# Two graph layers fused on one Trainium2 core: the order of work between the steps, where layer 1 begins, beside its matmuls and in the last rows

## The chip, the core and the metric

The kernel runs on one NeuronCore of a Trainium2 chip. Five engines run side by side, each with its own queue of instructions, taken in order: TensorE (PE) does the matmuls and the transposes, VectorE (DVE) and ScalarE (ACT) work on vectors, GpSimd (POOL) does small vector work, and SyncE (SP) issues DMA transfers. ACT and POOL issue transfers too. Engines wait for each other through semaphores. The metric is the device time of one execution in microseconds (us), as the median of several runs.

## The reference

A graph has N = 2708 nodes with D = 256 features and a random sparse adjacency `adj` (weights from 0.05 to 1, the diagonal set in the mask). Layer 0 adds two kinds of propagation, two steps each; layer 1 is a graph attention layer with four heads of 64 features. Both are followed by a layernorm with a residual.

```python
# layer 0
R = S + eye(N);  R = R / R.sum(-1, keepdims=True)
Z, Xf, Xa = 0, X, X
for n in range(2):
    A  = top_p_attention(Xa, W1, W2, W3)   # softmax(q @ k.T), the rows' largest entries
                                           # up to a mass of 0.9, renormalised
    Xf = R @ Xf
    Xa = A @ Xa
    Z  = Z + Xf @ U1[n].T + Xa @ U2[n].T
h = layernorm(X + Z) * ln_g + ln_b
x = layernorm(x + h)
# layer 1
Wh  = einsum('nd,hdo->nho', x, W)
e   = leaky_relu(s_i[:, None, :] + s_j[None, :, :], 0.2)   # s_i, s_j from Wh and a
att = softmax(where(adj != 0, e, -inf), axis=1)
x   = layernorm(x + einsum('ijh,jho->iho', att, Wh).reshape(N, 256))
```

## The kernel before

The nodes lie in NT = 22 row tiles: 16 of 128 rows and 6 of 110. All is float32. A fast way is computed always. A flag, `bad`, says at the end whether the data kept to the fast way's assumptions; if not, a general way follows inside `tc.If`. With this input it isn't entered.

**Layer 0.** For each tile there is a *walk* (`walks`, L901: 22 matmuls of one tile of the adjacency with `xe` or, in step 1, `xm`) into a single PSUM buffer, and an attention row: logits (`scores`, L661), a search for the top-p threshold on DVE, ACT and POOL (`search`: MAX8 at L766, MATCH_REPLACE8 at L786 and L832), turning the weights by PE transposes (`turned`, L240) with an ACT copy (L245), and the matmuls with them (`weigh`, L258). The end of a walk is an add on DVE that frees the PSUM buffer: `after_walk0` with `xf` (L915) in step 0, `finish` with `xw` (L974) in step 1. `step(s, ...)` goes over the 22 tiles of a step; between groups of source tiles it calls `slot`. A slot first advances the searches in progress (`going`) and the endings of earlier tiles (`doing`), and then issues a number of walk matmuls; `SPEND_BETWEEN` is 7 pieces of work of the stream. Between step 0 and step 1 there is a stretch of slots alone, in which the rest of step 0's walks and the first three searches of step 1 are done.

At the end of a tile of step 1, `finish` adds the terms, `norms` does the two layernorms, and `sources` computes what layer 1 needs of the tile: transposes (L160) and matmuls (L166) on PE, then `sb`, `tj`, `s_src` and `v` (the tile `cs`, L176) on ACT, and `v` goes to DRAM (L179). The last LATE = 4 tiles (18 to 21) have their norms and sources done later, beside layer 1's matmuls. For them a second form of the layernorm, `layernorm_beside`, has the sums made on ACT and one-column arithmetic on POOL (L146 to L151), and ACT applies it (L153). The multiply by the gain and the add of the residual are 256 wide on POOL (L187, L188).

**Layer 1.** The targets are taken in three groups of 8, 8 and 6 tiles (`spans`). For each group all 22 source tiles are gone over in pairs. Per source tile SP loads a block of the adjacency, ACT turns it into a mask (`neighbours`: Sign at L1221, Square at L1222), DVE sets the diagonal where the tile is among the targets (L1225), and DVE makes four weight tiles `pt`, one for each head (`weights`, L1302: one scalar_tensor_tensor of 1024 columns, three sets of buffers). PE then does 16 `values` matmuls per pair (L1313) and 16 `denominators` matmuls of `pt` with `sb` (L1323; counts for a group with two chunks of 512 columns). `beside` is called twice a pair, ahead of the values and behind the denominators. It advances the late tiles (`prepared`), `verdict` (which computes `bad` in some 17 small DVE operations, a matmul and a DVE operation) and the outputs of the group before (`settle`).

Once the last group is done, `settle` runs for its six tiles alone, in a staggered row: PE transposes (L1234), a reciprocal `rden` on DVE (L1236), the multiplication by it (odd tiles on DVE at L1242, even ones on ACT at L1247), the residual add on POOL (L1252), statistics on DVE (L1259 to L1261), the power and `nb` on POOL (L1262, L1263), the output on ACT (L1265), and the store. Then each engine loads the flag from `bad` (L1422) and branches (L1423).

From step 0 on the instructions of PE, ACT, DVE and POOL run in the order in which the program text issues them (`manual_schedule`); only SP's queue is put in order by the planner. So the place of a line in the text is its place in the engine's queue, and an instruction that waits holds up what is behind it.

Of the kernel before, what the change touches and what calls it, by code (L numbers as in the profile page):

```python
# [16 lines left out]
P = 128  # L17
# [27 lines left out]
def kernel(  # L45
# [71 lines left out]
    LATE = 4  # L117
# [63 lines left out]
    def norms(t, xt, norm=layernorm, other=None):  # L181

        m = rows[t]
        hh = xe[:m, t, 0:D]
        h2 = hh if other is None else other()[:m]
        yield from norm(h2, hh, m)
        nc.gpsimd.tensor_mul(h2, h2, g_sb[:m])  # L187
        nc.gpsimd.tensor_add(h2, h2, xt[:m])  # L188
        yield
        yield from norm(hh, h2, m)  # L190
        yield
        if t < NT - LATE:
            yield
# [23 lines left out]
    def spread(g, r):  # L217

        lines = shared[g].rearrange("(t h) m -> h t m", h=H)
        n = len(spans[g]) * rows[spans[g][0]]  # L220
        for k in range(2):
            for h in range(2):
                nc.sync.dma_start(
                    r[k][:, h, :n].rearrange("p (t m) -> p t m", t=len(spans[g])),
                    lines[2 * k + h].partition_broadcast(P),
                )

# [297 lines left out]
    def fast_layer0(ep, adjp):  # L525
# [463 lines left out]
        going, doing, unfinished, stored = [], [], set(), set()  # L989
        ready, held = {}, {}  # L990
# [8 lines left out]
        def slot(spend, begin=None):  # L999

            advance(going)
            if begin and begin[1] < NT:
                going.append(search(*begin))
                next(going[-1])
            advance(doing)
            owed[0] += spend
            while owed[0] > 0:
                owed[0] -= 1
                if next(stream, True):
                    break  # L1010

        def step(s, cur, spend):
            first = None
            for t in range(NT):
# [11 lines left out]
                def between(n):  # L1026
                    last = n == len(groups) - 1
                    if last:
                        xa = heldp.tile([P, D], F32, name="xa1")
                        nc.scalar.activation(xa[:m], ac[:m, :D], AF.Copy, scale=rden)  # L1030
                        if s and t in c3:
                            nc.gpsimd.dma_start(c3[t][:m], xa[:m])
                            stored.add(t)
                        elif s:
                            held[t] = xa
                        else:
                            doing.append(after_attention0(t, xa))
                    slot(spend[n], (s, t + 3) if n == len(groups) - 2 else None)

                def turn_next(n):  # L1040
# [5 lines left out]
                first = weigh(  # L1046
                    ac[:m, :D], first or turn_next(0), m,
# [46 lines left out]
        with tc.manual_schedule(engines=engines):  # L1094
# [22 lines left out]
            for t in range(3):  # L1117
                for n in range(6):
                    slot(SPEND_BETWEEN, None if n else (1, t))
                    if (t, n) == (2, 2):  # L1120
                        break
# [63 lines left out]
        return ahead, verdict  # L1185
# [7 lines left out]
    def layer1(ep, adjp, r=None, verdict=None):  # L1193
# [9 lines left out]

        first = list(range(GT, NT - LATE)) + list(range(GT)) + list(range(NT - LATE, NT))

# [7 lines left out]

        def neighbours(g, j):

            k = rows[j]
            i0, i1 = off[spans[g][0]], off[spans[g][-1] + 1]
            bar = adjp.tile([P, NT - HT, P], F32, name="blk")
            bar = bar.rearrange("p t d -> p (t d)")[:k, : i1 - i0]
            nc.sync.dma_start(bar, adjT[off[j] : off[j + 1], i0:i1])  # L1220
            nc.scalar.activation(bar, bar, AF.Sign)  # L1221
            nc.scalar.activation(bar, bar, AF.Square)  # L1222
            if j in spans[g]:
                own = bar[:, off[j] - i0 : off[j + 1] - i0]
                nc.vector.tensor_tensor(own, own, ident[:k, :k], op=ALU.max)  # L1225
            return bar

        def settle(g, t, val, den, u, last):
# [11 lines left out]
            sums = u[:m, 0:2, :].rearrange("p q (h o) -> p (q h) o", h=2)  # L1240
            if last and t % 2:
                nc.vector.tensor_tensor(  # L1242
                    res[:m], sums, rden[:m].unsqueeze(2).to_broadcast([m, H, FO]), op=ALU.mult
                )
# [6 lines left out]
            flat = res[:m].rearrange("p h o -> p (h o)")  # L1251
            nc.gpsimd.tensor_add(flat, flat, xe[:m, t, 0:D])  # L1252
# [33 lines left out]
        def mask(n):  # L1286
            if n < len(order):
                g, _, j = order[n]
                if g == 0:
                    nc.scalar.dma_start(  # L1290
                        v[j][: rows[j]].rearrange("p h o -> p (h o)"), vd[j][: rows[j]]
                    )
                masks[n] = neighbours(g, j)
# [36 lines left out]
        def prepared(t):  # L1330

            yield from norms(
                t, x_late[:, t - NT + LATE, :], layernorm_beside,
                lambda: pp.tile([P, D], F32, name="h2", bufs=4),
            )
# [4 lines left out]
        if verdict:  # L1340
            late += [[2 * k, prepared(NT - LATE + k)] for k in range(LATE)]
            late.append([2 * LATE, verdict(aux)])
        rest, running = [], []
        def beside(g, i):
# [25 lines left out]
        for n in range(0, len(order), 2):  # L1370
# [13 lines left out]
            for u in (n, n + 1):  # L1384
                for k in range(2):
                    values(u, (2 * k, 2 * k + 1))
                    if last and u > n:
                        for c, (c0, w) in enumerate(cuts[g]):
                            copy = nc.scalar.copy if c == 0 else nc.vector.tensor_copy
                            copy(val[:, k, c0 : c0 + w], acc[k][c][:, :w])  # L1390
            for u in (n, n + 1):
# [7 lines left out]
            else:  # L1399
                beside(g, i + 1)  # L1400
            weights(n + 3)
            mask(n + 4)
        assert not late

# [9 lines left out]

    with ExitStack() as both:
# [6 lines left out]
    flag = nc.values_load(bad[0:1, 0:1])  # L1422
    with tc.If(flag > 0):  # L1423
# [50 lines left out]
```

## Time and profile before

| | |
|---|---|
| Median of 3 runs | 1587.1 us (1586.86 to 1587.92) |
| Profiled execution | 1586.25 us |
| Its span, first to last instruction | 1584.4 us |
| Mean granted PE clock | 0.993 |
| PE busy | 1537.4 us, 97% |
| DVE busy | 1201.2 us, 76% |
| ACT busy | 799.5 us, 50% |
| POOL busy | 440.9 us, 28% |
| Step 0's rest and first searches of step 1 | about 466 to 514 us |
| Layer 1's first matmul | 1225.22 us |
| Layer 1's last matmul of the weights ends | 1561.66 us |

All numbers on the profile come from one profiled execution. The busy shares say which engine has least to spare. The list of waits has, for each pair of instruction and releaser, the sum of idle time, how often it came, and the longest. The chain follows the work that ended last back from releaser to releaser. In the rows of a stretch, the numbers in brackets count instructions, and the next column is the granted PE clock, where 1.00 is full speed. In the timeline a row has start, duration, engine, line, operation, tiles and shapes, and in square brackets the idle time before it.

### The profile page before, as it was taken

How to read it: one execution, taken by the hardware profiler on the slowest of the kernel's cores; microseconds unless marked ns; L12 is line 12 of the kernel's file. 1: busy time of each engine (PE TensorE's matmuls, PEld its weight loads, DVE VectorE, ACT ScalarE, POOL GpSimd, SP SyncE). 2: the span in 40 equal slices, each digit the busy share in tenths (PEclk: the TensorE clock that was granted, in tenths of full speed). 3: DMA queues.
4: the chain of work that ended last, by engine and by line, in shares of the span. 5: the costliest groups of instructions: out<-in, count | busy, mean ns of one | idle time of the engine just before them, and what ended most of it. 6: DMA issues, size and time to landing. Idle time of an engine off the chain costs nothing. (4 is left out here: it accounts for less than half of the span.)

```text
span 1584.4 us, 23826 instructions
## 1 busy us (share of the span) xinstructions
PE 1537.4 (97%) x8029; PEld 1036.2 (65%) x8029; DVE 1201.2 (76%) x3651; ACT 799.5 (50%) x1462; POOL 440.9 (28%) x884
## 2 busy tenths in 40 slices
PE   8999999999998999999999999999998989999994
PEld 4477777776776888787778788887786323333342
DVE  4686776777309767877779888888883888999895
ACT  3444444444345455555645566656643454456473
POOL 2200000100023122232223544444541750044133
PEclk9999999999999999999999999999999999999998
DMA  6100000000144333332333444333343335334231
GB/s 163 61 12 13 9 13 9 9 11 11 43 114 105 100 84 102 80 89 72 85 89 95 110 109 109 104 99 93 91 101 110 110 110 161 95 107 133 81 100 43
DMA packets 172495, 128.27 MB, mean 81 GB/s; under 512 B 44342, under 2 KB 161804, under 8 KB 172362
## 3 DMA queue, kind: packets, MB, share of 16 engines
q1 hardware_dynamic: 162000, 111.86, 26.4%
q0 software_dynamic: 3648, 9.26, 1.7%
q10 hardware_dynamic: 6714, 5.54, 1.1%
q8 instruction: 65, 1.06, 0.3%
q14 instruction: 68, 0.56, 0.1%
HBM read 111.78 MB, written 13.46 MB: 79 GB/s over the span
## 5 line engine op out<-in xcount | busy, mean ns | idle before, releaser
L245 ACT COPY eT<-tr 128x512 f32<-128x512 f32 (+5 forms) x264 | 141.3, 535 | 287.5 <-PE tr L240 284.9
L686 ACT ACTIVATE junk<-e,minus,rth 128x2708 bf16<-128x2708 f32 (+1 forms) x88 | 232.8, 2646 | 36.1 <-POOL rth L718 35.2
L258 PE MATMUL att<-xm,eT 128*128 128x256 f32 (+3 forms) x968 | 230.9, 380 | 0.4 <-ACT xa L1030 0.4
L258 PE MATMUL att<-ba,eT 128*128 128x256 f32 (+3 forms) x968 | 230.8, 379 | 0.3 <-ACT eT L245 0.2
L901 PE MATMUL walk<-xe,blk 128*128 128x257 f32 (+3 forms) x968 | 225.3, 384 | 5.0 <-DVE xf L915 5.0
L901 PE MATMUL walk<-xm,blk 128*128 128x256 f32 (+3 forms) x968 | 222.0, 380 | 1.0 <-DVE xw L974 1.0
L1313 PE MATMUL acc<-pt,v 128*64 128x512 f32 (+3 forms) x1056 | 213.7, 548 | 4.5 <-DVE pt L1302 4.1
L901 PEld LDWEIGHTS walk<-xe,blk 128*128 128x128 f32 (+3 forms) x968 | 178.5, 187 | 50.3 <-issue 12.6
L1302 DVE SCALAR_TENSOR_TENSOR pt<-e,tj,blk 128x1024 f32<-128x1024 f32 (+3 forms) x176 | 185.5, 1122 | 20.7 <-ACT blk L1222 16.0
L901 PEld LDWEIGHTS walk<-xm,blk 128*128 128x128 f32 (+3 forms) x968 | 177.7, 186 | 34.4 <-issue 4.9
L258 PEld LDWEIGHTS att<-xm,eT 128*128 128x128 f32 (+3 forms) x968 | 169.6, 186 | 22.1 <-ACT xa L1030 0.8
L258 PEld LDWEIGHTS att<-ba,eT 128*128 128x128 f32 (+3 forms) x968 | 169.5, 186 | 22.0 <-ACT eT L245 0.8
L665 ACT ACTIVATE e<-lg 128x1024 f32<-128x1024 f32 (+1 forms) x132 | 121.0, 921 | 110.6 <-PE lg L661 107.0
L1313 PEld LDWEIGHTS acc<-pt,v 128*64 128x64 f32 (+1 forms) x1056 | 74.7, 137 | 132.9 <-issue 109.4
L766 DVE MAX8 cand<-e 128x8 f32<-128x170 f32 (+1 forms) x352 | 89.6, 324 | 90.5 <-ACT e L665 90.4
L240 PEld LDWEIGHTS tr<-ident,e 128*128 128x128 f32 (+3 forms) x968 | 115.1, 138 | 56.3 <-issue 21.0
L240 PE MATMUL tr<-ident,e 128*128 128x128 f32 (+3 forms) x968 | 147.1, 271 | 0.7 <-ACT xe L952 0.3
L1302 DVE SCALAR_TENSOR_TENSOR pt<-r,tj,blk 128x1024 f32<-128x1024 f32 (+1 forms) x88 | 109.8, 1312 | 6.1 <-PE acc L1323 3.2
L1323 PE MATMUL acc<-pt,sb 128*32 128x512 f32 (+3 forms) x1056 | 106.8, 545 | 0.0
L766 DVE MAX8 cand<-scr 128x8 f32<-128x97 f32 (+1 forms) x616 | 102.3, 246 | 0.0
L915 DVE TENSOR_TENSOR xf<-walk,xe 128x257 f32<-128x257 f32 (+1 forms) x22 | 9.4, 426 | 110.6 <-PE walk L901 110.6
L784 DVE MAX8 top<-work 128x8 f32<-128x128 f32 (+3 forms) x242 | 82.4, 340 | 8.3
(237 smaller groups left out, 1966.9 us busy)
## 6 DMA issues: line engine op xcount, KB each, us to landing
blk<-in_adjT_dram SPq DMA_DIRECT2D x32, 704.0 KB
blk<-in_adjT_dram SPq DMA_DIRECT2D x32, 512.0 KB
blk<-in_adjT_dram SPq DMA_DIRECT2D x48, 330.0 KB
blk<-in_adjT_dram SPq DMA_DIRECT2D x32, 320.0 KB
blk<-in_adjT_dram SPq DMA_DIRECT2D x12, 605.0 KB
blk<-in_adjT_dram SPq DMA_DIRECT2D x12, 440.0 KB
blk<-in_adjT_dram SPq DMA_DIRECT2D x18, 283.6 KB
c<-cs POOLq DMA_DIRECT2D x32, 128.0 KB, 2.0
```

The costliest lines, as they stand in the source:

```text
L240: nc.tensor.transpose(tr[: rows[t], q, :m], e[:m, off[t] : off[t + 1]], ident[:m, :m])
L245: copy(eT[:k, : len(grp), :m], tr[:k, : len(grp), :m])
L258: nc.tensor.matmul(acc, eT[: rows[t], q, :m], value(t), start=(t == 0), stop=(t == NT - 1),)
L665: nc.scalar.activation(halves[:m, :, c0 : c0 + w], lg[:m, :, :w], AF.Exp, accum_out=zp[:m, n : n + 1],)
L686: nc.scalar.activation(junk[:m], e[:m], func, scale=rth, bias=minus1[:m], accum_out=acc)
L766: nc.vector.max(cand[:, n, :], src[:m, n * size : min(N, (n + 1) * size)])
L784: nc.vector.max(top[:, k : k + 8], work if k else flat)
L901: nc.tensor.matmul(ac[:m, :w], blk[: rows[j], j - j0, :m], cur[: rows[j], j, 0:w], start=(j == 0), stop=(j == NT - 1),)
L915: nc.vector.tensor_add(xf[:m], ac[:m, : D + 1], xe[:m, t, :])
L1302: nc.vector.scalar_tensor_tensor(pt[:k, :gw], targets[g][h // 2][:k, h % 2, :gw], tj[:k, j, h : h + 1], bar, op0=ALU.max, op1=ALU.mult,)
L1313: nc.tensor.matmul(acc[h // 2][c][q * FO : (q + 1) * FO, :w], v[j][:k, h, :], probs[n][h][:k, c0 : c0 + w], **at,)
L1323: nc.tensor.matmul(acc[2][c][h * 32 : (h + 1) * 32, :w], sb[:k, j, h : h + 1].to_broadcast([k, 32]), probs[n][h][:k, c0 : c0 + w], **at,)
```

## The change

1. **Between the steps.** `slot` has an argument `walk_first`. With it, the walk's matmuls are issued ahead of the searches' parts. It is set in the stretch between the steps.
2. **LATE is 3.** Tile 18 gets its norms and sources in layer 0.
3. **The first masks.** `neighbours` moves out of `layer1`, and the first two are called in the last tile of step 1. The loads of `v` for the first three source tiles go to SP's queue.
4. **The late tiles' norms** (`prepared`). Statistics, gain and residual are on DVE; the power alone is on POOL; `nb` is on DVE, three steps of `beside` later; ACT applies it.
5. **`beside`'s second call** in a pair comes between the values and the denominators.
6. **`verdict`** starts 26 steps of `beside` in (NT + 4) where it was 8.
7. **The last rows.** For odd tiles, the multiplication and the residual add are four scalar_tensor_tensor operations of 64 columns on DVE; POOL's add is left out for them.
8. **The flag** is loaded into registers inside `layer1`, ahead of the last rows on PE, ACT, DVE and POOL. SP's load isn't held in the written order.

```diff
-    LATE = 4
+    LATE = 3
...
-        def slot(spend, begin=None):
-            advance(going)
-            if begin and begin[1] < NT:
-                going.append(search(*begin))
-                next(going[-1])
-            advance(doing)
+        def slot(spend, begin=None, walk_first=False):
+            def search_parts():
+                advance(going)
+                if begin and begin[1] < NT:
+                    going.append(search(*begin))
+                    next(going[-1])
+                advance(doing)
+            if not walk_first:
+                search_parts()
             owed[0] += spend
             while owed[0] > 0:
                 owed[0] -= 1
                 if next(stream, True):
                     break
+            if walk_first:
+                search_parts()
...
+                    if s and (t, n) == (NT - 1, len(groups) - 2):
+                        early.extend(neighbours(0, j, adjp) for j in first[:2])
                     slot(spend[n], (s, t + 3) if n == len(groups) - 2 else None)
...
-                    slot(SPEND_BETWEEN, None if n else (1, t))
+                    slot(SPEND_BETWEEN, None if n else (1, t), True)
...
             if last and t % 2:
-                nc.vector.tensor_tensor(
-                    res[:m], sums, rden[:m].unsqueeze(2).to_broadcast([m, H, FO]), op=ALU.mult
-                )
+                for h in range(H):
+                    nc.vector.scalar_tensor_tensor(
+                        res[:m, h, :], sums[:, h, :], rden[:m, h : h + 1],
+                        xe[:m, t, h * FO : (h + 1) * FO], op0=ALU.mult, op1=ALU.add,
+                    )
...
-            nc.gpsimd.tensor_add(flat, flat, xe[:m, t, 0:D])
+            if not (last and t % 2):
+                nc.gpsimd.tensor_add(flat, flat, xe[:m, t, 0:D])
...
-                    nc.scalar.dma_start(
+                    (nc.sync if n < DEEP else nc.scalar).dma_start(
                         v[j][: rows[j]].rearrange("p h o -> p (h o)"), vd[j][: rows[j]]
                     )
-                masks[n] = neighbours(g, j)
+                masks[n] = early[n] if n < len(early) else neighbours(g, j, adjp)
...
         def prepared(t):
-            yield from norms(
-                t, x_late[:, t - NT + LATE, :], layernorm_beside,
-                lambda: pp.tile([P, D], F32, name="h2", bufs=4),
-            )
+            m = rows[t]
+            xt = x_late[:m, t - NT + LATE, :]
+            hh = xe[:m, t, 0:D]
+            h2 = pp.tile([P, D], F32, name="h2", bufs=LATE)[:m]
+            for src, dst in ((hh, h2), (h2, hh)):
+                if src is h2:
+                    nc.vector.tensor_mul(h2, h2, g_sb[:m])
+                    nc.vector.tensor_add(h2, h2, xt)
...
+                nc.vector.bn_stats(st, src)
+                nc.vector.bn_aggr(mv, st)
+                nc.vector.tensor_scalar(ve, mv[:, 1:2], LN_EPS, None, op0=ALU.add)
+                nc.gpsimd.tensor_tensor(rs, ve, minus_half[:m], op=ALU.pow)
+                yield
+                yield
+                yield
+                nc.vector.tensor_scalar(nb, mv[:, 0:1], rs, -1.0, op0=ALU.mult, op1=ALU.mult)
+                yield
+                nc.scalar.activation(dst, src, AF.Identity, scale=rs, bias=nb)
+                yield
             yield from sources(t, pp, aux, nc.scalar)
...
-            late.append([2 * LATE, verdict(aux)])
+            late.append([NT + 4, verdict(aux)])
...
+            if not last:
+                beside(g, i + 1)
             for u in (n, n + 1):
                 denominators(u)
...
-            else:
-                beside(g, i + 1)
             weights(n + 3)
             mask(n + 4)
         assert not late
+        if verdict:
+            flag.append(nc.values_load(bad[0:1, 0:1]))
...
-    flag = nc.values_load(bad[0:1, 0:1])
-    with tc.If(flag > 0):
+    with tc.If(flag[0] > 0):
```

## The prediction

> **What bounds the kernel now.** I read the page's busy shares first, then the list of waits, then the chain inside layer 1, then single stretches.
>
> ```profile
> PE 1537.4 (97%) x8029; PEld 1036.2 (65%) x8029; DVE 1201.2 (76%) x3651; ACT 799.5 (50%) x1462; POOL 440.9 (28%) x884
> ```
>
> TensorE (PE) sets the time: idle in only 47 us of 1584.4. A change can win only from PE's idle time, from PE running at a lower clock, from PE work removed, or from the tail behind the last matmul. The list of PE's waits shows which idle times the diff can touch:
>
> ```profile
> PE aux L160 <- ACT xe L153: 6.5, 3, 2.2
> PE walk L901 <- DVE xf L915: 5.0, 3, 3.2
> PE acc L1313 <- DVE pt L1302: 4.1, 1, 4.1
> ```
>
> 6.5 us three times 2.2, in layer 1's first group; 5.0 us between the steps (0.52, 1.31, 3.18 at 466.5, 489.5 and 503.5); 4.11 us once, where layer 0 passes to layer 1 (1221.11 to 1225.22). The chain shows how a 2.2 arises (start, us, what):
>
> ```profile
> 1269.74 3.57 PE acc L1323 x32
> 1273.32 1.09 PE aux L166 x4
> ...
> 1274.71 0.85 ACT cs L176 x4
> ...
> 1275.59 0.29 ACTq L179
> ...
> 1275.93 0.61 ACT xe L153
> ...
> 1276.58 0.41 PE aux L160 x2
> ```
>
> One tile's source matmuls (L166) come after the pair's denominators (L1323). Next on PE come the following tile's transposes (L160), whose rows ACT finishes (L153) only after the five small copies and the store of the tile before. PE stands idle from 1274.39 to 1276.58.
>
> Last, busy time by stretch (sum, PE, PEld, DVE, ACT, POOL, then PE's clock, DMA):
>
> ```profile
> 490.00:512.00 22.00, 18.00 (x73) 13.51 (x74) 21.13 (x81) 11.53 (x13) 6.87 (x15) 0.92 0.41 109
> 1225.00:1236.00 11.00, 10.65 (x40) 3.93 (x44) 11.00 (x11) 5.89 (x9) 1.47 (x2) 0.85 0.38 114
> 1328.00:1400.00 72.00, 72.00 (x425) 22.22 (x423) 67.91 (x63) 34.03 (x51) 4.42 (x7) 1.00 0.35 104
> ```
>
> After two gaps PE ran at half clock for 3.41 us (508.00 to 511.41, 1224.80 to 1228.21): some 1.7 us each. In group 1 PE is full and DVE has only 4 us in 72 to spare.
>
> **Between the steps: 3.6 us.** Each walk waits for the add (L915) that clears the one walk accumulator. Before, that add stands behind search parts on DVE, and a new walk follows on PE at once. With the walk put first in a slot, PE runs logits after three of the walk ends (1.99 us for 512 columns, 0.83 for 330), which cover an eviction of 0.5. By hand from these rows and a walk matmul of 0.4425 us, three waits remain: 0.52, about 0.5, and about 2.1 where the add falls into the replacing chain (seven MATCH_REPLACE8, 3.8 us, 494.15 to 497.96); together 3.1 in place of 5.0. The last lies between 0.5 (DVE free) and 4.6 (behind the 28 MAX8). So 1.9 are saved, and 1.7 of half clock if 2.1 keeps the clock. No walk matmul is added. The first search ends some 5 us later (506 for 501), still before its tile is turned. Bounds: -1 to +4.
>
> [...] the two throttles begin 716.8 us apart, 210 windows, so the edges are known. Window 504.59 to 508.00 was idle only 2.11 us and was throttled; window 1303.31 to 1306.72 was idle 1.83 and was not. [...] by the rows a 2.1 or 2.65 us gap may cost 1.7 according to its phase. I take none for the first and price the second below.
>
> **Layer change.** Tile 18's norms and sources move into layer 0 (LATE 3): PE gets 1.1 us there (L160 0.2, L166 0.9) and loses about 1.4 in group 0, in which one tile costs 0.34 + 1.09. DVE's added 2.3 us lie in its 4.08 us of idleness at 1191.15. POOL's order moves tile 19's sums by about 3.5 us, with nothing due on them; tile 18's store on SP goes ahead of the second mask load, about 2.4 us late and still landed near 1210, long before it is read. The Sign and Square of the first masks (four of 1.05 us) ran at 1221.70, after the last attention; now ACT does them during the last tile. A third mask's pair stands ahead of the last two turned copies: its load is issued after the last walk near 1213.1, landed near 1216.7 (3.5 us as the other masks), so PE may lose 0 to 0.2. v's loads for the first three tiles move from ACT's queue to SP's and wait, as before, for the end of attention. First weight then about 1222.45 for 1223.88; PE idle from 1222.3 to about 1224.95, 2.65 for 4.11.
>
> **Group 0.** The late tiles' norms go from ACT and POOL to DVE: a half is bn_stats 0.43, aggregate 0.18, add 0.15, later ln_nb 0.18, and the second has two 256-wide operations of 0.42 (as L1242): 2.75 us per tile, 8.3 for three. POOL keeps only the power; it loses the multiply and adds of 0.73, and ACT no longer waits 9.4 us for lb_nb. L166 comes before 3.57 us of denominators, which hide ACT's chain of 2.2: the three stalls, 6.5 us, go. What is late next is DVE: a weight has a pitch of 1.196 us, 8 per pair 9.57, against PE's 10.59 (values 7.02, denominators 3.57). Pairs 3 to 5 carry about 2, and 0.7 of diagonal maxima from then on. DVE's sum up to the sixth pair's weights is 1222.45 + 48 x 1.196 + 7.7 + 0.7 + 1.3 [...] = 1289.5. PE follows by 0.4 + 3.57 + 1.43, so pair 6 ends at about 1294.5, pair 7 (10.59 + 1.43) at 1306.3, pair 8 at 1318.0; before, it ended at 1327.92. So 9.9 us for layer change and group 0. A half clock in pair 1 mostly vanishes in this sum, as DVE sets it.
>
> [...]
>
> ```profile
> 1234.98 12.96 POOL L149 TENSOR_SCALAR lb_sq<-lb_sq 110x1 f32<-110x1 f32 x1 [6.13 <-ACT h L148]
> 1248.02 0.57 POOL L150 TENSOR_TENSOR lb_rs<-lb_sq,minus_half 110x1 f32<-110x1 f32 x1
> ...
> 1254.58 1.50 POOL L150 TENSOR_TENSOR lb_rs<-lb_sq,minus_half 110x1 f32<-110x1 f32 x1
> ```
>
> A one-element operation took 12.96 us while weights ran back to back, and finished when DVE paused. ln_nb on DVE now waits for such a power, with all later weights queued behind it and PE behind those. By the row the cover, three half pairs or 16 us, exceeds 12.96 and five of six cost nothing[...]. I take the 1.3 above and keep 0 to 4.
>
> **Group 1: -1.0.** The verdict (about 17 small DVE operations of 0.18 to 0.31, 3.7 us) moves to pairs 3 to 6 of group 1, where DVE has some 0.6 per pair and its lead: 0 to 2 lost.
>
> **Tail: 1.3.** Behind the last matmul (1561.66) POOL paces the six tiles:
>
> ```profile
> 1571.02 0.64 POOL L1252 TENSOR_TENSOR res<-res,xe 110x256 f32<-110x256 f32 x1
> 1571.61 0.55 POOL L1262 TENSOR_TENSOR ln_rs<-ln_ve,minus_half 110x1 f32<-110x1 f32 x1
> 1572.26 0.26 POOL L1263 TENSOR_SCALAR ln_nb<-ln_mv,ln_rs 110x1 f32<-110x1 f32 x1
> ```
>
> About 1.55 us a tile. Three adds of 0.7 go (2.1). DVE in exchange has four operations of 110x64 for one of 0.42; not in the trace, they lie between 0.17 (110x4) and 0.28 (the search's 128x56 of this kind). At 0.25, DVE's sum from 1562.8 is 6 x 0.85 + 3 x 1.0 plus waits, ending near 1571.3 for 1572.51: 1.2 saved, between 0 and 2. The span ends with POOL: its branch at 1573.82, a drain of 6.69 us to 1583.54. The flag's load on POOL (0.49, half of it on the path) is ahead now: 0.25 saved. On PE (0.49) it lies in the 0.6 us wait for den's copies, on ACT and DVE (0.66, 0.55) it may push rden by 0.15. SP's load stays, its chain done 2.6 us before POOL's. Together 1.3.
>
> **Sum.** 3.6 + 9.9 - 1.0 + 1.3 = 13.8. The profiled execution took 1586.25 (span 1584.4, 1.85 around it), 0.85 under the median 1587.1; taken off the median: **1573.3 us**.
>
> **The rivals.**
> 1. DVE becomes layer 1's bound more than summed: powers at 0.66 each (2.7 over my 1.3), verdict 2.0. For it: 94% busy DVE in group 1, the 12.96. Against it: the cover. About 1578.
> 2. Between the steps nothing is won: the adds fall behind MAX8 chains, the half clock stays. For it: DVE busy 21.13 of 22. Time 1577.
> 3. No change within 0.2%: DVE's pause costs in group 0 what the L160 stalls did, and the tail is fixed by a drain that doesn't move: 1585 to 1588.
> 4. Slower: the ln_nb waits. If POOL's power isn't served while DVE waits for it, or its queue is late, each of the six stops DVE, and PE with it. It decides from 13.8/6 = 2.3 us each; at 3 us, 1591. Against it: POOL has little else left there, and the power took 0.57 with DVE paused.
> 5. Better than summed: weights stretch less without POOL's 256-wide work, clock kept throughout: 1567.
>
> **How the numbers follow.** As summed, 0.63, with its own range 1569 to 1577; rival 1 0.18, rival 2 0.08, rival 3 0.03, rival 4 0.03, rival 5 0.05. 0.2% (3.2 us) is about what a measurement of this kernel can tell from no change. The range reaches to rival 1 with two costs at their bounds and to rival 5: 1567 to 1581. Faster 0.94 (all but 3 and 4), same 0.03, slower 0.03.
>
> **What would show it.** The L160 wait gone from PE's list; walk waits near 3 us; one wait of about 2.6 at the layer change, with or without a half clock; pair 8's end near 1318 less the earlier gains; PE waits on L1302 in pairs 4 to 6 of 2 to 3 us; POOL's branch about 1.5 us sooner behind the last matmul. Wrong if DVE waits for ln_rs by microseconds, if group 1 shows PE waiting for weights in every pair, or if the last turned copies wait for the third mask.

## The result, and the profile after

The changed kernel takes 1576.47 us (median of 4 runs, 1574.92 to 1576.54), the kernel before beside it 1587.34 us: a ratio of 0.9929, with a 95% interval from 0.9912 to 0.9946. On another chip it took 1574.76 us, ratio 0.9926 (0.9913 to 0.9940). So 11 us were won where 13.8 had been forecast, and the time lies inside the range of 1567 to 1581. The changed kernel's nine runs lie either at 1574.3 to 1574.9 us or at 1576.4 to 1577.0, by PE's granted clock (see the last section), so smaller differences between kernels are read here from traces. The profiled execution took 1574.92 us, its span 1573.1 us, which is 11.3 us below the span before.

The change adds lines ahead of the ones the forecast spoke of: the walk is L916 now (L901 before), the attention matmul L273 (L258), the turned copy L260 (L245), the weights L1314 (L1302), the values L1325 (L1313), the denominators L1335 (L1323).

The page's busy shares after:

```profile
PE 1536.7 (98%) x8029; PEld 1037.0 (66%) x8029; DVE 1208.0 (77%) x3698; ACT 791.8 (50%) x1428; POOL 411.9 (26%) x850
```

and the head of the list of PE's waits (us in total, times, longest):

```profile
PE tr L625 <- DMA xa<-in_w1T_dram: 4.9, 1, 4.9
PE att L273 <- ACT eT L260: 3.8, 1, 3.8
PE acc L1325 <- DVE pt L1314: 2.7, 1, 2.7
PE walk L916 <- DVE xf L930: 2.3, 3, 1.3
```

The three waits for L153 are gone (6.5), the layer change fell from 4.1 to 2.7, and the walks' waits from 5.0 to 2.3, which is less than the 3.1 forecast. The first line is the load of the weights at the start, 4.8 us before. The second is a wait that was not there before: the first attention matmul of step 1 waits 3.8 us for its turned copy. PE's busy time hardly changed, so all of this is a matter of waits, of the clock and of the rows behind the last matmul.

Where the time moved shows best at points that both traces have (us from the span's start, PE unless said otherwise; the last pair's end is that of its last matmul in the timeline, 0.2 us behind the 1561.66 of the forecast, where the chain leaves it):

| point | before | after | after less before |
|---|---|---|---|
| first walk's end between the steps | 466.53 | 465.63 | -0.90 |
| a walk's wait in mid step 1 begins | 903.54 | 903.46 | -0.08 |
| last attention matmul's end | 1221.11 | 1222.97 | +1.86 |
| layer 1's first matmul | 1225.22 | 1225.67 | +0.45 |
| pair 8 ends | 1327.92 | 1320.15 | -7.77 |
| pair 33, the last, ends | 1561.86 | 1554.38 | -7.48 |
| POOL's branch | 1573.82 | 1564.73 | -9.09 |
| POOL's drain begins | 1576.85 | 1565.29 | -11.56 |
| span ends | 1584.4 | 1573.1 | -11.3 |

The 0.9 us at the start lie in the first 20 us (loads of the weights and PE's slow first stretch: a matmul of `lg` with `ident` took 0.42 us in it and 0.27 behind it, in both traces, and the records of PE's clock, which begin with full speed, begin at 13.07 before and at 11.23 after); nothing of the change is there, and in the repeat of the changed kernel the same point came at 466.61, so this part is a difference from run to run. Between the steps 0.8 us were lost, not 3.6 won: from the first walk's end to the wait in mid step 1 it took 437.0 us before and 437.8 after, and 439.0 in the repeat, where the half clock that follows lasted twice as long. The stretch from the middle of step 1 to the end of pair 8 brought 7.7, the last rows 3.8.

### The profile page after: what moved, and what is told of

Its sections match the earlier page's. It is cut to its first block, busy times and chain, and to the rows that moved or that the text cites. A ratio compares the mean times of both kernels' runs of the same rounds, so it can differ in the third digit from the quotient of the medians.

```text
span 1573.1 us, 23768 instructions
## 1 busy us (share of the span) xinstructions
PE 1536.7 (98%) x8029; PEld 1037.0 (66%) x8029; DVE 1208.0 (77%) x3698; ACT 791.8 (50%) x1428; POOL 411.9 (26%) x850
## 4 chain that ended last, share of the span: by engine, by line
PE 92%; DVE 4%; ACT 1%; POOL 1%; issue 1%; DMA 0%; ACTq 0%; POOLq 0%; DVEq 0%
PE att L273 25%; PE walk L916 25%; PE acc L1325 13%; PE lg L676 7%; PE acc L1335 7%; PE tr L255 6%; PE tr L961 2%; PE tr L975 2%; PE tr L646 1%; PE tr L166 1%; DVE pt L1314 1%; ACT junk L701 1%; DVE scr L847 0%; DVE scr L766 0%; PE aux L1242 0%
## 5 line engine op out<-in xcount | busy, mean ns | idle before, releaser
L260 ACT COPY eT<-tr 128x512 f32<-128x512 f32 (+5 forms) x264 | 141.2, 535 | 276.9 <-PE tr L255 274.3
L701 ACT ACTIVATE junk<-e,minus,rth 128x2708 bf16<-128x2708 f32 (+1 forms) x88 | 232.8, 2646 | 35.9 <-POOL rth L733 35.1
L273 PE MATMUL att<-ba,eT 128*128 128x256 f32 (+3 forms) x968 | 231.3, 380 | 3.8 <-ACT eT L260 3.8
L273 PE MATMUL att<-xm,eT 128*128 128x256 f32 (+3 forms) x968 | 230.9, 380 | 0.4 <-ACT xa L1052 0.4
L916 PE MATMUL walk<-xe,blk 128*128 128x257 f32 (+3 forms) x968 | 224.9, 384 | 2.3 <-DVE xf L930 2.3
L916 PE MATMUL walk<-xm,blk 128*128 128x256 f32 (+3 forms) x968 | 222.0, 380 | 1.5 <-DVE xw L989 1.5
L1325 PE MATMUL acc<-pt,v 128*64 128x512 f32 (+3 forms) x1056 | 214.0, 549 | 2.9 <-DVE pt L1314 2.7
L916 PEld LDWEIGHTS walk<-xe,blk 128*128 128x128 f32 (+3 forms) x968 | 178.3, 186 | 47.6 <-issue 12.0
L916 PEld LDWEIGHTS walk<-xm,blk 128*128 128x128 f32 (+3 forms) x968 | 177.6, 186 | 35.1 <-issue 4.9
L1314 DVE SCALAR_TENSOR_TENSOR pt<-e,tj,blk 128x1024 f32<-128x1024 f32 (+3 forms) x176 | 184.4, 1113 | 13.6 <-PE att L273 8.7
L273 PEld LDWEIGHTS att<-ba,eT 128*128 128x128 f32 (+3 forms) x968 | 169.6, 186 | 25.6 <-ACT eT L260 4.3
L273 PEld LDWEIGHTS att<-xm,eT 128*128 128x128 f32 (+3 forms) x968 | 169.6, 186 | 22.1 <-ACT xa L1052 0.8
L1325 PEld LDWEIGHTS acc<-pt,v 128*64 128x64 f32 (+1 forms) x1056 | 75.7, 137 | 132.0 <-issue 108.3
L1314 DVE SCALAR_TENSOR_TENSOR pt<-r,tj,blk 128x1024 f32<-128x1024 f32 (+1 forms) x88 | 109.8, 1311 | 3.0 <-PE acc L1335 1.3
L1335 PE MATMUL acc<-pt,sb 128*32 128x512 f32 (+3 forms) x1056 | 106.8, 545 | 0.0
L236 ACT ACTIVATE blk<-blk 128x1024 f32<-128x1024 f32 (+3 forms) x66 | 63.3, 958 | 81.4 <-DMA blk<-in_adjT_dram 66.6
L930 DVE TENSOR_TENSOR xf<-walk,xe 128x257 f32<-128x257 f32 (+1 forms) x22 | 9.4, 426 | 117.0 <-PE walk L916 117.0
```

The source lines that it names most:

```text
L260: copy(eT[:k, : len(grp), :m], tr[:k, : len(grp), :m])
L273: nc.tensor.matmul(acc, eT[: rows[t], q, :m], value(t), start=(t == 0), stop=(t == NT - 1),)
L701: nc.scalar.activation(junk[:m], e[:m], func, scale=rth, bias=minus1[:m], accum_out=acc)
L916: nc.tensor.matmul(ac[:m, :w], blk[: rows[j], j - j0, :m], cur[: rows[j], j, 0:w], start=(j == 0), stop=(j == NT - 1),)
L1314: nc.vector.scalar_tensor_tensor(pt[:k, :gw], targets[g][h // 2][:k, h % 2, :gw], tj[:k, j, h : h + 1], bar, op0=ALU.max, op1=ALU.mult,)
L1325: nc.tensor.matmul(acc[h // 2][c][q * FO : (q + 1) * FO, :w], v[j][:k, h, :], probs[n][h][:k, c0 : c0 + w], **at,)
```

## The experiments

**The slots between the steps.** The changed kernel with this part undone:

```diff
-                    slot(SPEND_BETWEEN, None if n else (1, t), True)
+                    slot(SPEND_BETWEEN, None if n else (1, t))
```

> The changed kernel with the slots between the steps in the old order (searches' parts ahead of the walk). Theory (the walk-first order saves 2.7 us of walk waits and the half clock behind them, and gives 3.75 us and a half clock back where the first turned copy of step 1 stands behind a search's pass on ACT): the waits 0.5, 1.3 and 3.2 us for L930 come back, the wait of PE for the turned copy goes, and the time is 0.8 us lower than the changed kernel's, about 1575.6. Rival (the order pays, and the turned copy is late for another reason): the 3.75 us wait stays and the time is 2 to 4 us above, 1578.5 to 1580.5.

It took 1574.58 us (1574.35 to 1575.14), ratio to before 0.9922 (0.9905 to 0.9938). The waits for L930 are back at 5.0 in total, and the 3.8 us wait for the turned copy is gone. So the wait belongs to the new order, and the new order costs at least as much as it wins: from the first walk's end to mid step 1 this kernel took 437.0 us, as before. Whether the cost is the 0.8 us of the traces, the times alone can't tell.

The chain of the changed kernel between 507 and 515 shows what holds the copy up (start, us, what):

```profile
507.14 0.82 ACT e L680 x2
...
508.09 2.17 POOL fact L688
...
511.28 0.40 ACT rth L718
...
511.70 2.74 ACT junk L701 x2
514.44 0.48 ACT eT L260
...
514.96 2.41 PE att L273 x8
```

With the walk first, parts of the searches stand behind the last slot's matmuls, directly ahead of step 1. One of these parts is a pass over a whole row on ACT (`tally`, L701), which waits for a small chain on POOL. ACT takes its instructions in order, so the two copies for step 1's first tile, ready to go at 511.2, wait for POOL and then for the pass. PE has nothing else to do and stands from 511.21 to 514.96. Then comes a half clock, from 516.40 to 519.81.

If that is the cause, the parts of the last slot need only come after the copies. The next kernel lets the last slot issue its walk alone; its parts follow in step 1's first slot:

```diff
-        def slot(spend, begin=None, walk_first=False):
+        def slot(spend, begin=None, walk_first=False, parts=True):
...
-            if walk_first:
+            if walk_first and parts:
                 search_parts()
...
-                    slot(SPEND_BETWEEN, None if n else (1, t), True)
+                    slot(SPEND_BETWEEN, None if n else (1, t), True, (t, n) != (2, 2))
```

> The changed kernel in which the last slot between the steps issues its walk alone; the searches' parts of that slot come in step 1's first slot, behind the first turned copies. Theory: PE's wait for the turned copy (3.75 us at 511) falls under 1 us, no half clock follows, step 1 begins 4 to 5 us sooner, and the time is about 1571.7. Rival (the pass on ACT only moves in front of the next turned copy): the wait appears at the third copy with 2 us or more, gain under 2 us, 1575.

It took 1571.34 us (1570.75 to 1572.15), ratio 0.9901 (0.9885 to 0.9918). Its timeline (start, us, engine, line, operation, tiles, shapes, count, idle before) has the copies ahead of the pass, and PE idle for only 0.24 us:

```profile
511.10 1.07 ACT L260 COPY eT<-tr 128x512 f32<-128x512 f32 x2 [2.86 <-PE tr L255]
512.05 0.40 ACT L718 ACTIVATE rth<-slope,nguess,y 128x1 f32<-128x1 f32 x1
512.49 2.64 ACT L701 ACTIVATE junk<-e,minus,rth 128x2708 bf16<-128x2708 f32 x1
```

```profile
511.74 1.99 PE L273 MATMUL att<-ba,eT 128*128 128x256 f32 x8 [0.24 <-ACT eT L260]
```

The walks' waits stay at 2.3, no half clock follows, and layer 1 begins at 1220.59 in place of 1225.67. From the first walk's end to mid step 1 it took 432.6 us, 4.4 less than before: this is what the forecast, at 3.6, had meant for this part. At the end 1.0 us is lost again, since POOL's branch took 1.65 us here (see below).

**The parts of layer 1's first group, one by one.** Four kernels, measured by one quantity that neither the start nor the tail touches: from layer 1's first matmul to the end of pair 11. Before it is 134.46 us, in the changed kernel 126.25. The quantity has a spread of its own: six other traces with the changed kernel's group 0 lie at 126.2 to 126.4, but the kernel before with only the flag moved took 136.18, since a half clock, 1.7 us, followed one of its waits for L160.

`beside_only` is the kernel before with one edit:

```diff
+            if not last:
+                beside(g, i + 1)
             for u in (n, n + 1):
                 denominators(u)
...
-            else:
-                beside(g, i + 1)
```

> The kernel before with the second call of beside ahead of the denominators and nothing else. Theory (each L160 stall is ACT's chain between two tiles, which 3.57 us of denominators cover): the three waits of 2.2 us for ACT xe L153 fall below 0.3 each, the loss of 2.1 us in pair 3 stays, and the time is 6.5 us lower, 1580.5. Rival (ACT is late for its wait on POOL, so the waits only move): half of it or less, 1583.5 or above.

1580.75 us, ratio 0.9962 (0.9948 to 0.9976). No wait for L153 is left. The stretch took 129.76 us, 4.7 less: of the 6.5 of stalls, 2.1 came back in pair 9 (12.67 us in place of 10.59), where DVE waits for a mask that ACT makes late, as in pair 3. DVE's waits between 1225 and 1345:

```profile
DVE pt L1302 <- ACT blk L1222: 4.6, 2, 4.1
DVE blk L1225 <- ACT blk L1222: 4.5, 2, 4.1
```

Of the 5.8 us between the two profiled executions, 1.2 are the start's run-to-run difference. The time fits the theory, the sum within it only in part.

`prepared_only` is the kernel before with the new `prepared` alone, four late tiles, `beside` in its old place.

> The kernel before with the late tiles' norms on DVE (four tiles) and nothing else. Theory: pair 3 no longer loses 2.1 us, as DVE's weights don't wait for a mask held up on ACT; the L160 waits stay, one for each pair of tiles, with 1.5 to 2.2 us; DVE's extra 11 us lie inside them. 2 us lower, 1585. Rival (DVE becomes the bound by this part alone): PE waits for the weights in pairs 4 to 7 by over 3 us beside the L160 waits, and the time is 1587 or above.

1587.56 us, ratio 1.0001 (0.9992 to 1.0010). The stretch took 138.82 us, 4.4 more than before, of which 1.7 is a half clock that followed one of the waits for L160: these three waits stay, pair 3 is at PE's pace as the theory had it, but pairs 4 to 6 take 11.4 to 13.1 us each, at DVE's pace. The rival holds. That the time is no worse comes from the tail, told of below.

`both_only` is the kernel before with both.

> The kernel before with the norms on DVE and beside ahead of the denominators, without the other parts (LATE stays 4, masks late). Theory (the gain of layer 1's first group comes from these two alone, less what DVE's bound takes): no L160 waits, 2 to 4 us lost to weights in pairs 4 to 8, 6 to 7 us lower than before, 1580.5. Since DVE carries four tiles in place of three and starts 1.4 us later than with early masks, it stays 1 to 2 us short of the 7.8 us which the changed kernel wins there. Rival (LATE or the masks bring most of it): under 4 us, 1583 or above.

1580.60 us, ratio 0.9958 (0.9944 to 0.9972); the stretch 131.67 us, 2.8 less than before, though 1.9 more than with `beside` alone. Both traces have the same half clock in pair 1 and none later. The norms on DVE cost more than they were moved to save.

`old_norms` asks the same from the other side: the changed kernel, three late tiles and all else, with `prepared` as it was (and `norms` with the arguments that it needs).

```diff
-            m = rows[t]
-            xt = x_late[:m, t - NT + LATE, :]
...
-                nc.scalar.activation(dst, src, AF.Identity, scale=rs, bias=nb)
-                yield
+            yield from norms(
+                t, x_late[:, t - NT + LATE, :], layernorm_beside,
+                lambda: pp.tile([P, D], F32, name="h2", bufs=4),
+            )
```

> The changed kernel with the late tiles' norms as before (sums on ACT, one-column work and the 256-wide operations on POOL, application on ACT), still three tiles and beside ahead of the denominators. Theory (on DVE the norms cost 2.4 us of waits for weights in pairs 4 to 6; on ACT and POOL they hold two masks up by 2.1 us each): from the end of pair 1 to that of pair 11 about 114.5 us in place of 112.7, pairs 4 to 6 at PE's pace, two others 2.1 us long; 1.9 us slower at that point. POOL's stream is longer, so its branch may take 2.9 us again and add 2.1. Rival (the move to DVE brings nothing, DVE is the bound because of it): pair 11 ends 1 us or more sooner than in the changed kernel.

1574.29 us, ratio 0.9921 (0.9904 to 0.9937); the stretch 125.76 us, 0.5 below the changed kernel. I had expected 1.9 more; it is the rival that comes nearer. DVE's waits between 1239 and 1330, first of the changed kernel:

```profile
DVE blk L240 <- ACT blk L237: 2.4, 1, 2.4
DVE pt L1314 <- PE acc L1335: 1.3, 1, 1.3
```

and of the kernel with the old norms:

```profile
DVE pt L1316 <- PE acc L1337: 4.3, 3, 2.1
DVE blk L242 <- ACT blk L239: 3.6, 1, 3.6
DVE pt L1316 <- ACT cs L176: 1.2, 1, 1.2
```

DVE has 9.1 us of slack in place of 3.7, and PE loses 1.6 us in one pair (pair 9, 12.16 us), where DVE waits for a late mask. With the other parts in place, the norms' engine makes next to no difference. Of the 5.4 us between `both_only` and the changed kernel, the third late tile, the later verdict and the earlier first weights have not been told apart.

`masks_late` takes the two early masks out of the last tile:

```diff
                     if s and (t, n) == (NT - 1, len(groups) - 2):
-                        early.extend(neighbours(0, j, adjp) for j in first[:2])
+                        pass
```

> The changed kernel with its first masks made in layer 1 as before (loads and all else as changed). Theory (DVE's start sets the end of group 0): ACT's Sign and Square of mask 0 come behind attention, DVE's first weight starts 2 us later, near 1225, and pair 8 ends as much later as DVE starts: 1.5 to 2.5 us above the changed kernel, 1578.5. Rival (the first matmul waits for v's load and ACT's copy anyway, and PE sets the group): under 0.5 us, 1576.5.

1574.29 us, ratio 0.9919 (0.9903 to 0.9936). Both theories miss. The trace shows ACT making the first two masks in the last tile all the same, at 1210.63 and 1216.39, which is even sooner than in the changed kernel (1217.51 and 1220.58). So the written order holds inside layer 0 and inside layer 1, but ACT's first work of layer 1 stood ahead of layer 0's last copies here: across that border ACT did not keep the order of the text, which the description of the kernel gives for everything from step 0 on. The two lines in the last tile add nothing: from the first matmul to pair 11 the kernel took 126.37 us. In the kernel before, the load of `v` on ACT's queue came ahead of the first mask, at 1221.15, and waited for the end of attention; that its move to SP's queue is what frees the masks is likely, and was not tried alone. The first matmul came 2.56 us after attention, by this row:

```profile
PE acc L1325 <- DMA v<-v: 2.6, 1, 2.6
```

The load of `v` is issued when attention ends, and here its landing is what the layer change waits for. In the changed kernel the list names the weights instead; but the first weight was done at 1224.35, 1.3 us before the first matmul, so that `v` is the likely cause there too.

**The last rows and the branch.** POOL's branch took 2.94 us to POOL's next instruction before, 0.47 after. The forecast had the branch unchanged. The branch and the next instruction (duration in ns, first and last start in us), first before, then after:

```profile
L1423 POOLq COMPARE_BRANCH  x1: 45/45/45, 1573.8 to 1573.8; - x1
L1423 POOLq EVENT_SEMAPHORE  x1: 17/17/17, 1576.8 to 1576.8; - x1
```

```profile
L1457 POOLq COMPARE_BRANCH  x1: 45/45/45, 1564.7 to 1564.7; - x1
L1457 POOLq EVENT_SEMAPHORE  x1: 17/17/17, 1565.2 to 1565.2; - x1
```

Two kernels ask why. One is the kernel before with the flag's load moved up, the other the changed kernel with 34 small POOL instructions more at the start.

```diff
         assert not late
+        if verdict:
+            flag.append(nc.values_load(bad[0:1, 0:1]))
...
-    flag = nc.values_load(bad[0:1, 0:1])
-    with tc.If(flag > 0):
+    with tc.If(flag[0] > 0):
```

> The kernel before with the flag's load ahead of the last rows and nothing else. Theory A (POOL's branch was quick in the changed kernel because its instructions lie at other places in the stream): the branch on POOL still takes 2.9 us to the next instruction, the gain is the load alone, 0.2 to 0.3 us, 1587. Theory B (the early load makes the branch quick): the branch takes 0.5 us, POOL's drain starts 2.7 us sooner, and the time is 1584.5.

1586.68 us, ratio 0.9997 (0.9988 to 1.0006), no change that can be told. The branch took 3.07 us.

```diff
     LATE = 3
+    filler = const.tile([P, 1], F32, name="filler")
+    for _ in range(34):
+        nc.gpsimd.memset(filler, 0.0)
```

> The changed kernel with 34 one-column memsets on POOL at the start, as many instructions as its POOL stream is shorter by. Theory A (place in the stream): POOL's branch takes 2.9 us again in place of 0.47, POOL's drain ends the program again, and the time is 2.1 us above the changed kernel's (2.5 less the 0.38 that POOL waits for SP's end), 1578.6. Theory B (the early load): the branch stays at 0.5 us and the time within 0.5 us, 1576.5.

1578.25 us, ratio 0.9942 (0.9925 to 0.9958); the branch took 2.83 us again, and from the last matmul to the span's end it took 20.8 us in place of 18.8. So the early load has no part in it: with 34 instructions more at the start of POOL's stream the branch went from 0.47 us to 2.83. By which place in the stream this goes was not told apart. All runs, by the number of POOL records ahead of the branch:

| kernels | POOL records ahead of the branch | branch to next, us |
|---|---|---|
| defer | 1093 | 1.65 |
| after, masks_late, slots_old, settle_old | 1094 to 1097 | 0.47 |
| prepared_only, both_only | 1102 | 0.47 |
| combined, old_norms | 1116 and 1117 | 0.47 to 0.48 |
| pad34, flag_only, before, beside_only | 1128 to 1131 | 2.83 to 3.07 |

Records are not quite instructions (`defer` and the changed kernel have the same 850 busy POOL instructions), so the one record between 1093 and 1094 doesn't say where the step lies.

The short branch is what kept `prepared_only` near the kernel before: 4.4 us lost in layer 1, 2.5 won at the branch and 0.6 ahead of layer 1.

Last, the changed kernel with the odd tiles of the last rows as before:

```diff
-                for h in range(H):
-                    nc.vector.scalar_tensor_tensor(
-                        res[:m, h, :], sums[:, h, :], rden[:m, h : h + 1],
-                        xe[:m, t, h * FO : (h + 1) * FO], op0=ALU.mult, op1=ALU.add,
-                    )
+                nc.vector.tensor_tensor(
+                    res[:m], sums, rden[:m].unsqueeze(2).to_broadcast([m, H, FO]), op=ALU.mult
+                )
...
-            if not (last and t % 2):
+            if True:
                 nc.gpsimd.tensor_add(flat, flat, xe[:m, t, 0:D])
```

> The changed kernel with the last rows' odd tiles as before (one multiplication on DVE, the residual add on POOL). Theory (POOL paced the last rows at 1.55 us a tile, DVE paces them now): from the last weight's matmul to POOL's branch 11.6 us in place of 10.35, with POOL's idle time gone; 1.1 us slower, 1577.5, if the branch itself takes 0.5 us. Rival (the output's two buffers pace the last rows, since the last output on ACT waits for an earlier store): under 0.3 us, 1576.5.

1575.06 us, ratio 0.9930 (0.9913 to 0.9946): not to be told from the changed kernel by its time. In the trace POOL's branch came 11.39 us behind the last values or denominators matmul in place of 10.35, and the span's end 19.5 in place of 18.8. The part is worth 1.0 us at POOL. At the end it is worth 0.7 between these two traces, but six traces with the new rows and the short branch end 18.45 to 19.12 us behind the last matmul, so 0.3 to 1.0. The rival has a share in this: in the changed kernel POOL's drain ends at 1571.98, and POOL then waits until 1572.35 for SP, whose last store waits for ACT's last output, and that for an earlier store to land:

```profile
1566.70 0.60 ACT L1277 ACTIVATE o<-res,ln_nb,ln_rs 110x256 f32<-110x256 f32 x1 [1.86 <-DMA out_dram<-o]
```

With the old rows this wait is 0.54 us. So part of what POOL gains is handed to the stores.

**What did better alone, together.** The walk alone in the last slot, the masks left to layer 1, the norms on ACT and POOL; the changed kernel ran beside it.

> The changed kernel with three edits that did better alone: the last slot between the steps issues its walk alone, the first masks are made in layer 1's text, and the late tiles' norms are on ACT and POOL. Theory (the three lie in different stretches and add up: 4.3, 0.3 and 1.0 us by the traces): a span of about 1567.5, the time 1569.5, 5 us or more below the changed kernel on the same chip. Rival (on ACT the norms and masks now meet, and the masks' hold-ups take back what the norms gain): at the time of the last-slot edit alone, 1571.3.

> The changed kernel itself, for a comparison on one chip: 1575 to 1577, POOL's branch 0.47 us, the wait for the turned copy 3.75 us.

Together: 1569.28 us (1568.35 to 1570.26), ratio to before 0.9891 (0.9876 to 0.9906); the changed kernel beside it 1574.76 (1574.26 to 1576.96). This is the best of all, 5.5 us below the changed kernel and 18 below the kernel before. Most of it is the last slot's edit. Its profiled span is 2.7 us below that of `defer`: 0.9 is the start, 1.0 the branch (0.47 us for 1.65), and only about 0.8 lies between the steps' end and the end of group 0, where the other two edits act. By their times alone neither of these could be told from the changed kernel. The head of its list of PE's waits:

```profile
PE tr L627 <- DMA xa<-in_w1T_dram: 4.7, 1, 4.7
PE walk L918 <- DVE xf L932: 2.3, 3, 1.3
PE acc L1327 <- DMA v<-v: 2.2, 1, 2.2
```

## Why the prediction was right, and where its steps were not

The time and its sign were right. Of the parts, one had the wrong sign (between the steps, 4.4 us too high), group 0 was 2.2 us too high, and the tail was 2.5 too low. That these pulled in opposite ways, and that the start gave 0.9 us, is luck.

**Between the steps: the step that failed.** "The first search ends some 5 us later (506 for 501), still before its tile is turned" is all that the forecast says of what stands behind the moved parts, and it looks at DVE alone. The walks' waits came out as worked out, only better (0.52, 0.52, 1.28 for 0.52, 0.5, 2.1). But each search part issues to ACT as well, and the pass that the last slot issues lands in front of step 1's first copies. That gave 3.75 us and a half clock back: -0.8 in place of +3.6. `defer` shows it, by changing nothing but the order: +4.4.

**Layer change: right in the gap, wrong in its start.** PE's gap was forecast at 2.65 us and measured at 2.70. Attention ended 0.7 us later than forecast (1222.97 for 1222.3): beside tile 18's 1.1 us there is a wait of 0.53 at 1180.45 for a walk's add (L989) that the forecast didn't have. The first weight followed attention's end by 0.1 us, as the forecast had it (1223.07 for 1222.45).

**The half clock in pair 1: right.** The forecast said that it would mostly vanish, since DVE sets the pace there. The changed kernel had it, the kernel with the old slots had not, and both took 13.5 us from the first matmul to the end of pair 1. Busy time by stretch, the PE clock before the last two columns, first of the changed kernel, then of the one with the old slots:

```profile
1225.50:1239.30 13.80, 13.50 (x66) 4.69 (x68) 13.73 (x15) 3.70 (x4) 3.81 (x3) 0.88 0.34 99
```

```profile
1224.70:1238.40 13.70, 12.87 (x66) 3.73 (x68) 13.63 (x14) 3.83 (x4) 3.72 (x3) 1.00 0.30 95
```

A clock of 0.88 for 1.00, and the same time; DVE is busy for 13.73 of 13.80 us and for 13.63 of 13.70.

**Group 0: DVE's sum right, PE's distance behind it not.** The 48th weight ended at 1289.42, forecast 1289.5. Pair 6 ended at 1296.16 for 1294.5, pair 8 at 1320.15 for 1318.0, 2.15 us late, so that layer change and group 0 brought 7.7 for 9.9. Nearly half of this is a slip in the sum: 1289.5 + 0.4 + 3.57 + 1.43 is 1294.9, not 1294.5, and two more pairs of 10.59 + 1.43 make 1319.0, not 1318.0. The rest is PE's distance: it came 6.7 us behind the 48th weight and not 5.4, since its values ended 2.0 us behind that weight and not 0.4. The chain there:

```profile
1283.76 7.64 PE acc L1325 x32
1291.40 1.07 PE aux L166 x4
1292.48 0.11 PE aux L208
1292.59 3.57 PE acc L1335 x32
```

In pairs 4 to 6 late weights cost PE some 1.1, 0.4 and 0.6 us, 2.1 in all, as forecast; that PE was held up this early, and once late does not catch up, fits the greater distance, and was not tried alone. Pairs 7 and 8 took 12.00 each, as forecast. The forecast's 1.3 us for POOL's powers, with 0 to 4 as their range, was an estimate. One power took 5.23 us here, the others 1.45 to 1.58, and 0.55 each in the last rows, but DVE never waited for one.

```profile
1255.24 1.54 POOL L1358 TENSOR_TENSOR ln_rs<-ln_ve,minus_half 110x1 f32<-110x1 f32 x1 [8.91 <-DVE ln_ve L1357]
1261.70 5.23 POOL L1358 TENSOR_TENSOR ln_rs<-ln_ve,minus_half 110x1 f32<-110x1 f32 x1 [4.92 <-DVE ln_ve L1357]
```

What POOL did cost lay elsewhere: two weights at 1225.46 and 1227.13 took 1.74 us in place of 1.28 while POOL ran two 256-wide adds of the last tile.

```profile
1225.27 0.86 POOL L996 TENSOR_TENSOR xe<-xe,xa 110x256 f32<-110x256 f32 x1 [9.26 <-ACT xa L1052]
1226.09 1.70 POOL L997 TENSOR_TENSOR x_late<-x_late,b_sb 110x256 f32<-110x256 f32 x1
```

What the forecast ascribed to the norms' move, however, isn't there: alone it cost 2.7 us (and a half clock), beside `beside`'s new place 1.9, and with all other parts 0.5. The gain of this group is that of `beside`'s place, of one late tile fewer, and of DVE being rid of the verdict and starting sooner, in shares that stay open for the last three.

**Group 1:** -1.0 forecast, -0.3 measured, in one pair (11.38 us for 11.06).

**Tail: right in direction, mis-sized by the branch.** Forecast 1.3, measured 3.8 at the span's end. POOL's branch came 1.6 us sooner behind the last matmul (forecast about 1.5); of this the flag's load is 0.55 (11.95 to 11.40 in `flag_only`), the rows 1.0. The other 2.5 are the branch's own time, which the forecast had taken as fixed. Of these 4.1 us, 0.4 are lost to POOL's wait for SP; put back alone (`pad34`), the long branch costs 2.0. DVE's part came as summed: its last operation ended 9.5 us behind the last matmul for 10.65 before, 1.2 saved. POOL's timeline shows the rows' new pace, powers 0.87 apart where no add lies between:

```profile
1562.40 0.55 POOL L1274 TENSOR_TENSOR ln_rs<-ln_ve,minus_half 110x1 f32<-110x1 f32 x1
1563.05 0.27 POOL L1275 TENSOR_SCALAR ln_nb<-ln_mv,ln_rs 110x1 f32<-110x1 f32 x1
1563.27 0.55 POOL L1274 TENSOR_TENSOR ln_rs<-ln_ve,minus_half 110x1 f32<-110x1 f32 x1
```

Four of the DVE operations of 110x64, which no row of the trace before had, took 0.86 us together, close to the 0.25 each that was taken.

So the sum stands as 0.9 from the start, -0.8, 7.7, -0.3 and 3.8: 11.3. Without the branch's luck (2.0 to 2.5) and with the start as before it would have been near 8.

## What to carry to other kernels

When a block of work is moved in a queue that is kept in order, list what it issues on every engine, and look at each engine for the next instruction that PE waits for; a saving of 2.7 us of one wait can come back as another of 3.75 on an engine that the moved wait never touched. When a gain is measured, take it apart at common points of the two traces before giving it to the edits: here 2.0 to 2.5 us came from the time of one branch, which changed with the number of instructions ahead of it, and a part that cost some 3 us looked harmless for the same reason. An engine that sets the pace can hide a slower clock of another, as DVE did here in pair 1, with 13.5 us at a PE clock of 0.88 and at 1.00: check which one is continuously busy before counting a stretch at half clock as lost.

## What the runs showed of the hardware

POOL's branch took 2.83 to 3.07 us to POOL's next instruction in the runs with 1128 to 1131 records ahead of it, 0.47 to 0.48 with 1094 to 1117, and 1.65 in the one with 1093. Why is not shown. The other engines' branches took 2.6 to 3.9 us before and 2.5 to 4.0 after.

In the traces of the kernels before and after, each stretch of half clock between the steps and at the layer change lasted 3.41 us. Counted from the first, the two later ones of each trace (the third lies behind the last matmul) began a whole number of such lengths on: 210 and 311 before, 208 and 306 after. Cut into windows of 3.41 us from there, with PE's idle time added up in each (matmul ends as the profile models them) and from the window ahead of the first half clock on, the two traces have six windows at full clock with 1.97 us or more of idle time, and half clock followed each:

| trace | window begins | idle, us | half clock begins |
|---|---|---|---|
| before | 504.59 | 2.11 | 508.00 |
| before | 1221.38 | 3.41 | 1224.80 |
| before | 1566.13 | 3.41 | 1569.55 |
| after | 512.99 | 1.97 | 516.40 |
| after | 1222.96 | 2.70 | 1226.37 |
| after | 1557.46 | 3.41 | 1560.88 |

Five windows, all of the kernel before, were idle for 1.00 to 1.86 us, and full clock followed each; all the others were idle for less. In `prepared_only` half clock followed a window with 1.73 us, so the two traces do not give a limit. Full clock came back behind windows at half clock with 0 to 0.42 us of idle time.

The same wait of 3.75 us went with 3.41 us of half clock in one run of the changed kernel (516.40 to 519.81) and with 6.82 in another (514.95 to 521.77). The kernel's runs fit this: of its nine, the four with a mean clock of 0.994 took 1574.26 to 1574.92 us, the five with 0.993 took 1576.42 to 1576.96, and the two that were traced, one from each group, are these two. Half of 3.41 us, 1.7, is an estimate of what such a stretch costs where PE sets the pace; it accounts for most of that step.
